# An issue order on VectorE: the second token tile's convolution taps behind the chain of its step sizes

## The chip, the cores and the metric

The kernel runs on one core of one Trainium2 chip. Its time is the device time of one execution in microseconds, given as the median of several runs. A profile is a separate execution recorded by the hardware profiler; its times are counted from the start of its span.

## What is computed

One layer of a perceiver with 256 tokens of width 512, in float32 throughout. Three blocks follow each other, each on the layer norm of the running sum x and added back to it:

```python
x = x + xattn(layernorm(x), ctx)   # attention: 16 heads over 4096 context positions and the tokens themselves
x = x + ssd(layernorm(x))          # a state space block (below)
x = x + moe(layernorm(x))          # 32 experts, 6 of them for each token, and a shared expert
```

The change lies in the second block. Cut to what matters:

```python
zxbcdt = u @ W_in.T                       # z: 1024, xBC: 1280, dt: 16 columns
xBC = silu(causal_conv(xBC, conv_w) + b)  # 4 taps along the tokens, for each of 1280 channels
dt  = softplus(dt + dt_bias)              # the step sizes: one for each token and head
A   = -exp(A_log)
dA  = dt * A;  A_cs = cumsum(dA)          # running sums inside a chunk of 128 tokens
L   = tril(exp(A_cs[l] - A_cs[s]))        # decays between two tokens of a chunk
Y   = ((C B^T) * L) @ (x dt) + C state * exp(A_cs) + x * D
y   = rmsnorm(Y * silu(z)) * norm_weight
out = y @ W_out.T
```

## The kernel before

The 256 tokens are two tiles of 128, which are the two chunks of the state space block. Attention takes about the first 720 us. The first token tile's part of the state space block up to the decays runs beside the end of attention; the second tile's part begins when its attention output has been projected and normalized, at about 737 us. The expert stage starts at about 805 us and runs to the end.

The kernel is written in a tile framework. The program names tiles and operations; the framework adds the semaphores and lays out, once at build time, the order in which each engine issues its instructions. It goes by the order of the program as priority, by the dependencies, by the free buffers, and by its own estimate of when each input is there. So an instruction that is late in the program can stand ahead of an earlier one that it expects to be not ready. `tc.issue_after(ins)` adds an order without a wait: what the block traces on the engine of `ins` is issued behind `ins` on that engine. On other engines it says nothing. On the chip each engine then works through its queue in that order.

The parts around the change, for token tile t:

- `steps_of(t)` makes the step sizes, on tiles of 128 x 16. `product` (lines 993 to 1000) turns the normalized tokens on TensorE, multiplies for dt, and prepares exp(-|v|). `series` (1002 to 1013) is the softplus as a chain of small VectorE instructions, each on the result of the one before: lines 1003 to 1007, six times line 1009, then 1010, 1012 and 1013. The last one writes dA. `sums` (1015 to 1024) makes the running sums by a matmul with a triangle (`ps_cs`) and copies them (line 1021).
- `decays(t)` spreads the sums: `ps_csT` is the transposed running sum, ScalarE copies it to `csT` and writes it to DRAM (`sums_d`), and GpSimd's queue reads it back to all partitions as `lm` (line 1039), and for the second tile also as `e1` (1043). Then come 16 subtractions on VectorE (line 1047) and the exponentials on ScalarE (1051, 1053).
- `channels(t)` is the convolution, by ten channel tiles `ct` of 128. TensorE makes a piece (`ps_xbc`); ScalarE copies it to `xraw` (1067) and writes the last tap with the bias into `y` (1068). The other three taps add to `y`: for ct 3 and 7 by ScalarE and GpSimd (1073, 1074), for the other eight by VectorE (line 1076, one instruction of 128 x 128 for each tap). `active` (1079) is the SiLU over all ten.
- `gates(t)` makes z (`ps_z`) and its SiLU on ScalarE (1091). `mixing`, `within`, `carried` and `assemble` make Y, and `mamba_out` multiplies by W_out and normalizes. `turn_xn` (234, `lnT`) turns the normalized tokens for the next block.

PSUM tiles come from three tags in a fixed rotation (`bank`): mm with two banks, sc with three, tp with one.

For the second tile the program traces, in this order:

```python
product()
series()
lm = decays(1)
run(chans[1][c] for c in order[0:3])   # channel tiles 8, 9, 0
sums()
lm[0]()                                # spread the sums
run(chans[1][c] for c in order[3:])    # channel tiles 1 to 7
run(gates(0))
run(lm[1:])                            # line 1047 and the exponentials
hold(*w_x, lacc[:, 0], behind=decay_begun[-1])
```

`hold` starts loads of expert weights on SyncE's queue (line 1427), behind the first instruction of line 1047.

Of the kernel before, what the change touches and what calls it, by code (L numbers as in the profile page):

```python
# [15 lines left out]
ALU = mybir.AluOpType  # L16
# [3 lines left out]
P = 128  # L20
# [64 lines left out]
def perceiver_layer(ctx: ExitStack, tc: tile.TileContext, a: dict, out: bass.AP):  # L85
    nc = tc.nc
    V, S, G, TE = nc.vector, nc.scalar, nc.gpsimd, nc.tensor
# [69 lines left out]
    def layer(ctx, bounded):  # L157
# [73 lines left out]
        def turn_xn(t, tp, halves=False):  # L231

            for k in range(KD):
                TE.transpose(tp[:, k * P:(k + 1) * P], xn[:, t, k * P:(k + 1) * P], ident)

            for copy, ks in (((V.tensor_copy, slice(0, KD // 2)), (S.copy, slice(KD // 2, KD))) if halves else
                             ((V.tensor_copy, slice(0, KD)),)):
                turned = copy(xT[:, ks, t * P:(t + 1) * P], tp.rearrange("p (k n) -> p k n", k=KD)[:, ks])
            return turned

        def project(ps, lhs, rhs_of):

            for k in range(KD):
                last = TE.matmul(ps, lhs(k), rhs_of(k), start=(k == 0), stop=(k == KD - 1))  # L244
            return last
# [692 lines left out]
        m = {}  # L938
        banks = ring([(ps_mm, "mm")])

        def bank(name):
            p, tag = banks()
            return p.tile([P, 512], FP, tag=tag, name=name)
# [44 lines left out]
        def steps_of(t):  # L988


            vdt, nab, u, z, z2, ser, dt, dA, acs = (m[n, t] for n in ("vdt", "nab", "u", "z", "z2", "ser", "dt", "dA", "acs"))

            def product():
                turn_xn(t, bank("lnT"), halves=True)
                ps = bank("ps_dt")
                project(ps[:, 0:SH], lambda k: xT[:, k, tok(t)], lambda k: m["w_bcd"][:, k, 256:272])
                V.tensor_tensor(vdt, ps[:, 0:SH], dt_bias, ALU.add)
                V.tensor_scalar(nab, vdt, -1.0, None, ALU.mult)
                V.tensor_tensor(nab, nab, vdt, ALU.min)
                S.activation(u, nab, AF.Exp)  # L1000

            def series():
                V.tensor_scalar(z, u, 2.0, None, ALU.add)
                V.reciprocal(z, z)
                V.tensor_tensor(z, z, u, ALU.mult)
                V.tensor_tensor(z2, z, z, ALU.mult)
                V.tensor_scalar(ser, z2, 1.0 / 15.0, None, ALU.mult)
                for d in (13, 11, 9, 7, 5, 3):
                    V.scalar_tensor_tensor(ser, ser, 1.0 / d, z2, ALU.add, ALU.mult)
                V.scalar_tensor_tensor(ser, ser, 1.0, z, ALU.add, ALU.mult)  # L1010
                V.tensor_scalar(vdt, vdt, 0.0, None, ALU.max)
                V.scalar_tensor_tensor(dt, ser, 2.0, vdt, ALU.mult, ALU.add)
                V.scalar_tensor_tensor(dA, dt, -1.0, m["ea", 0], ALU.mult, ALU.mult)

            def sums():

                ps = bank("ps_cs")
                TE.matmul(ps[:, 0:SH], upper, dA, start=True, stop=True)
                if t == 0:
                    TE.matmul(ps[:, SH:2 * SH], ones, dA, start=True, stop=True)  # L1020
                V.tensor_copy(acs, ps[:, 0:SH])
                if t == 0:
                    V.tensor_tensor(m["decay", 0], ps[:, SH:2 * SH], acs, ALU.subtract)
                    S.activation(m["decay", 0], m["decay", 0], AF.Exp)
            return product, series, sums

        decay_begun = []

        def decays(t):

# [25 lines left out]
        def channels(t):  # L1056


            xc, xraw = m["xc", t], m["xraw"]

            def piece(ct):
                w, c0 = ((w_x[ct // 4], ct % 4 * P) if ct < 8 else (m["w_bcd"], (ct - 8) * P))
                ps = bank("ps_xbc")[:, 0:P]
                project(ps, lambda k: w[:, k, c0:c0 + P], lambda k: xT[:, k, tok(t)])
                xb = xraw[:, ct, :]
                y = xc[:, ct, :]
                S.copy(xb[:, CONV - 1:], ps)
                S.activation(y, ps, AF.Identity, bias=conv_b[:, ct:ct + 1], scale=conv_w[:, ct, CONV - 1:CONV])
                for j in range(CONV - 1):
                    w = conv_w[:, ct, j:j + 1]  # L1070
                    if ct % 4 == 3:
                        tap = small.tile([P, P], FP, tag="tap", name="tap", bufs=2)
                        S.activation(tap, xb[:, j:j + P], AF.Copy, scale=w)
                        G.tensor_tensor(y, y, tap, ALU.add)
                    else:
                        V.scalar_tensor_tensor(y, xb[:, j:j + P], w, y, ALU.mult, ALU.add)

            def active():
                S.activation(xc, xc, AF.Silu)
                if t + 1 < NT:  # L1080
                    G.tensor_copy(xraw[:, :, 0:CONV - 1], xraw[:, :, P:P + CONV - 1])
            return [lambda ct=ct: piece(ct) for ct in range(XCT)], active
# [801 lines left out]
    with tc.If(flag == 1) as arms:  # L1884
        with ExitStack() as lctx:
            layer(lctx, True)
    with arms.Else():
        with ExitStack() as lctx:
            layer(lctx, False)
# [48 lines left out]
```

## Time and profile before

| what | value |
|---|---|
| median of 3 runs | 938.96 us (938.9 to 939.3) |
| the profiled execution | 939.45 us |
| its span | 937.7 us |
| TensorE busy | 924.1 us (99%) |
| VectorE busy | 579.2 us (62%) |
| ScalarE busy | 371.2 us (40%) |
| GpSimd busy | 428.3 us (46%) |
| mean granted TensorE clock | 0.998 of full speed |

In the profile PE is TensorE's matmuls and PEld its weight loads, DVE is VectorE, ACT is ScalarE, POOL is GpSimd, SP is SyncE; a q behind a name is that engine's queue of DMA issues. A float32 matmul shows as two records. A timeline line gives start, duration, engine, line, operation, out<-in by the program's names, shapes and count, and in brackets the idle time before it and what ended it. Several of the program's names share one buffer, so the 128 x 16 tiles of `steps_of` are shown as `xc`, `xraw` as `lacc`, and `e1` and z as `wkv`.

### The profile page before, as it was taken

To read this page: it belongs to the slowest core of one execution; us is meant where nothing else is said; L and a number is where in the kernel's file an instruction comes from. 1 tells how busy PE (TensorE), PEld (TensorE's weight loads), DVE (VectorE), ACT (ScalarE), POOL (GpSimd) and SP (SyncE) were. 2 spreads that over 40 slices of the span, in tenths; PEclk is the share of its full clock that TensorE was granted. 3 is DMA by queue.
4 is the path that set the end of the run, shared out by engine and by line. 5 is a ranking of instruction groups with operands and counts; after the bars stand their busy time and mean duration, and the time that the engine had idled before them with its cause. 6 is when DMAs were issued, how large, how long until landed. Compare 5 with 4: busy or idle time off the path is not lost.

```text
span 937.7 us, 10601 instructions
## 1 busy us (share of the span) xinstructions
PE 924.1 (99%) x3280; PEld 506.6 (54%) x3280; DVE 579.2 (62%) x1199; ACT 371.2 (40%) x855; POOL 428.3 (46%) x499
## 2 busy tenths in 40 slices
PE   9999999999999999999999999999999999999997
PEld 4444555555555555555555555554455695654332
DVE  4966756566665665655656666657589595662224
ACT  4556444444444343444444444434236362122211
POOL 3768855345544634725634554220003341455552
PEclk9999999999999999999999999999999999999999
DMA  9651053043015104305303401280016393689993
GB/s 335 203 113 59 0 180 89 1 129 108 12 35 179 34 12 146 91 1 157 91 0 106 109 12 35 67 268 35 0 43 200 136 332 113 233 284 352 420 392 106
DMA packets 129733, 122.33 MB, mean 130 GB/s; under 512 B 79906, under 2 KB 99139, under 8 KB 124419
## 3 DMA queue, kind: packets, MB, share of 16 engines
q1 hardware_dynamic: 118976, 77.43, 27.6%
q0 software_dynamic: 7504, 39.59, 11.4%
q10 hardware_dynamic: 3186, 4.54, 1.3%
q8 instruction: 28, 0.46, 0.2%
q14 instruction: 39, 0.31, 0.1%
HBM read 89.54 MB, written 32.00 MB: 130 GB/s over the span
## 4 chain that ended last, share of the span: by engine, by line
PE 90%; DMA 4%; DVE 4%; issue 1%; POOL 1%; ACT 0%; ACTq 0%; POOLq 0%; DVEq 0%
PE oT L787 24%; PE scT L761 24%; PE ps_kv L531 16%; PE ps_self L244 4%; PE ps_o L982 3%; PE ps_first L406 2%; PE ps_egu L244 2%; DMA xg_sb<-xd,listed 2%; DMA w_in<-in_experts_dram,place 2%; PE ps_egu L1651 1%; PE ps_xbc L244 1%; PE total L1692 1%; PE ps_ye L1722 1%; PE xgTp L1623 1%; PE ps_sgu L244 1%
## 5 line engine op out<-in xcount | busy, mean ns | idle before, releaser
L778 DVE TENSOR_TENSOR lacc<-lacc,prT 128x512 f32<-128x512 f32 x256 | 199.5, 780 | 198.4 <-ACT prT L767 197.4
L767 ACT ACTIVATE prT<-scT,bq,rk 128x512 f32<-128x512 f32 x256 | 198.5, 775 | 280.7 <-PE scT L761 269.6
L761 PE MATMUL scT<-qT,kT 128*128 128x512 f32 x536 | 273.5, 592 | 0.0
L787 PE MATMUL oT<-prT,v 128*128 128x512 f32 x528 | 269.4, 592 | 0.0
L787 PEld LDWEIGHTS oT<-prT,v 128*128 128x128 f32 x528 | 100.2, 190 | 125.3 <-issue 118.6
L761 PEld LDWEIGHTS scT<-qT,kT 128*128 128x128 f32 x536 | 101.3, 190 | 41.4 <-issue 30.8
L531 PE MATMUL ps_kv<-fast,ctx 128*128 128x256 f32 x350 | 99.5, 379 | 0.0
L531 PEld LDWEIGHTS ps_kv<-fast,ctx 128*128 128x128 f32 x350 | 66.5, 190 | 47.9 <-issue 40.2
L480 POOL TENSOR_TENSOR ctx<-ctx 128x128 f32<-128x128 f32 x21 | 10.4, 497 | 98.7 <-PE ps_kv L531 98.7
L218 POOL TENSOR_TENSOR rk<-pv,mhalf 128x4 f32<-128x4 f32 x32 | 38.4, 1211 | 27.3 <-DVE pv L217 27.1
L531 PE MATMUL ps_kv<-wkv,ctx 128*128 128x256 f32 x168 | 48.8, 379 | 0.0
L289 ACT ACTIVATE xn<-kraw 128x128 f32<-128x128 f32 x112 | 33.4, 300 | 38.6 <-POOL kraw L506 21.5
L516 POOL TENSOR_TENSOR v<-fast,v 128x768 f32<-128x768 f32 x21 | 40.9, 1959 | 16.2 <-DVE fast L560 15.6
L531 PEld LDWEIGHTS ps_kv<-wkv,ctx 128*128 128x128 f32 x168 | 31.9, 190 | 28.2 <-issue 24.4
L793 DVE TENSOR_TENSOR oacc<-oT,oacc 128x512 f32<-128x512 f32 x64 | 43.7, 682 | 0.0
L1415 POOL DMA_INDIRECT xg_sb<-xd,listed x21 | 20.4, 974 | 36.2 <-DVE lacc L1271 14.3
L531 PE MATMUL ps_kv<-fast,fast 128*128 128x256 f32 x112 | 33.3, 379 | 0.0
L531 PEld LDWEIGHTS ps_kv<-fast,fast 128*128 128x128 f32 x112 | 21.3, 190 | 17.8 <-issue 12.0
L295 DVE STREAM_TRANSPOSE tr<-kraw 128x512 f32<-128x512 f32 x28 | 18.3, 690 | 19.7 <-POOL kraw L505 19.7
L478 POOL TENSOR_TENSOR ctx<-fast 128x128 f32<-128x128 f32 x28 | 20.4, 730 | 19.5 <-PE ps_kv L531 19.1
L982 PE MATMUL ps_o<-wo,qT 128*128 128x512 f32 x64 | 28.8, 592 | 0.0
L244 PE MATMUL ps_self<-wq,xT 128*128 128x512 f32 x64 | 28.6, 592 | 0.0
(430 smaller groups left out, 1379.4 us busy)
## 6 DMA issues: line engine op xcount, KB each, us to landing
xg<-xn SPq DMA_DIRECT2D x6, 2560.0 KB, 9.1
ctx<-in_ctxT_dram SPq DMA_DIRECT2D x7, 1024.0 KB, 4.8
kd<-tr SPq DMA_DIRECT2D x112, 64.0 KB, 2.3
kT<-kd SPq DMA_DIRECT2D x28, 256.0 KB, 2.9
wq<-in_wq_dram SPq DMA_DIRECT2D x4, 1024.0 KB, 14.5
wo<-in_wo_dram SPq DMA_DIRECT2D x4, 1024.0 KB, 6.5
w_in<-in_W_inT_dram SPq DMA_DIRECT2D x4, 1024.0 KB, 5.0
w_in<-in_experts_dram SPq DMA_DIRECT2D x4, 1024.0 KB, 4.8
```

What stands on the lines that cost most here:

```text
L218: return G.tensor_tensor(dst, v[:, :n], mhalf[:, :n], ALU.pow)
L244: last = TE.matmul(ps, lhs(k), rhs_of(k), start=(k == 0), stop=(k == KD - 1))
L289: S.activation(sq[:, h, :], raw[:, h, :], AF.Square, accum_out=ss[:, h:h + 1])
L478: G.tensor_tensor(s1, x[:, 1, 0], x[:, 1, 1], ALU.add)
L516: G.tensor_tensor(to[:, 1:4], q, base[:, 1:4], ALU.add)
L531: TE.matmul(b[n], sets[name][i], y, start=start, stop=True, skip_group_check=True)
L761: scored.append(TE.matmul(sc, kT[:, g, i * P:(i + 1) * P], qT[:, t, heads4(g), :].rearrange("p h q -> p (h q)"), start=True, stop=True).ins)
L767: S.activation(pr, sc, AF.Exp, bias=shift, scale=SCALE if r is None else r[:, i, g:g + 1])
L778: V.tensor_tensor(la, la, pr, ALU.add)
L787: TE.matmul(outs[g, t], v[:, i, g * HD:(g + 1) * HD], pr, start=(n == 0), stop=last)
L793: V.tensor_tensor(ov, outs.pop((g, t)), ov, ALU.add)
L982: TE.matmul(m["ps_o", t], aT[:, t, h, :], wo[j][:, h % 4, :], start=(h == 0), stop=(h == NH - 1))
```

## The change

The instruction that writes dA is kept by its tile, and the VectorE taps of the second tile (t > 0) are traced inside `issue_after` of it. Nothing else is changed: the same instructions, the same data, the same buffers. The taps of ct 3 and 7 are outside of the block.

```diff
-                V.scalar_tensor_tensor(dA, dt, -1.0, m["ea", 0], ALU.mult, ALU.mult)
+                stepped[t] = V.scalar_tensor_tensor(dA, dt, -1.0, m["ea", 0], ALU.mult, ALU.mult).ins
...
-        decay_begun = []
+        decay_begun, stepped = [], {}
...
                     else:
-                        V.scalar_tensor_tensor(y, xb[:, j:j + P], w, y, ALU.mult, ALU.add)
+                        with tc.issue_after(stepped[t]) if t > 0 else nullcontext():
+                            V.scalar_tensor_tensor(y, xb[:, j:j + P], w, y, ALU.mult, ALU.add)
```

## The prediction

> **What bounds the kernel now.** I read the page first. TensorE (PE) is busy 924.1 of 937.7 us at the full granted clock, so only PE's idle time can be won, and what makes PE wait longer is lost. Next I read the chain of waits from 732 us on, where the second token tile's step sizes are made:
>
> ```profile
> 745.29 0.32 DVE xc L1013
> 745.65 0.40 PE ps_cs L1018 x2
> 746.05 0.32 PE ps_csT L1036 x2
> 746.37 2.00 PE ps_xbc L244 x16
> 748.37 0.22 issue
> 748.59 5.30 DMA lm<-sums
> 753.91 3.42 DVE lm L1047 x16
> ```
>
> (Start, duration, what.) The chain runs through dA (line 1013), two small matmuls, the round trip of the running sums through DRAM, and the 16 subtractions of line 1047. It then stays on VectorE (DVE) and GpSimd (POOL) up to the transposes at 780.89. DVE's own timeline in front of it shows what shares the queue with the series:
>
> ```profile
> 741.71 0.17 DVE L1006 TENSOR_TENSOR xc<-xc 128x16 f32<-128x16 f32 x1
> 741.83 0.35 DVE L1076 SCALAR_TENSOR_TENSOR xc<-lacc,by_channel,xc 128x128 f32<-128x128 f32 x1
> 742.10 0.17 DVE L1007 TENSOR_SCALAR xc<-xc 128x16 f32<-128x16 f32 x1
> ...
> 743.99 0.62 DVE L1076 SCALAR_TENSOR_TENSOR xc<-lacc,by_channel,xc 128x128 f32<-128x128 f32 x1
> 744.53 0.16 DVE L1009 SCALAR_TENSOR_TENSOR xc<-xc 128x16 f32<-128x16 f32 x1
> ...
> 746.09 0.17 DVE L1021 COPY xc<-ps_cs 128x16 f32<-128x16 f32 x1 [0.49 <-PE ps_cs L1018]
> 748.16 5.40 DVE L1076 SCALAR_TENSOR_TENSOR xc<-lacc,by_channel,xc 128x128 f32<-128x128 f32 x15 [1.90 <-ACT xc L1068]
> ```
>
> Nine of the tile's 24 VectorE taps (channel tiles 8, 9 and 0) sit one by one between the steps of the series; the other 15 run in a row before line 1047. Between the two groups DVE idles 2.4 us. Last, PE's timeline, which says how much a shorter chain can be worth:
>
> ```profile
> 743.69 1.38 PE L244 MATMUL ps_z<-xT,w_in 128*128 128x128 f32 x10 [0.72 <-ACT xc L1068]
> 745.65 0.40 PE L1018 MATMUL ps_cs<-xc,upper 128*128 128x16 f32 x2 [0.58 <-DVE xc L1013]
> ```
> ```profile
> 780.89 0.63 PE L234 MATMUL lnT<-ident,xn 128*128 128x128 f32 x4 [0.29 <-DVE xn L228]
> ```
> ```profile
> 746.00:758.00 12.00, 12.00 (x107) 11.79 (x107) 9.28 (x34) 8.05 (x20) 4.09 (x7) 1.00 0.65 209
> 758.00:770.00 12.00, 12.00 (x123) 11.71 (x122) 10.98 (x14) 8.53 (x12) 7.43 (x7) 1.00 0.91 352
> ```
>
> In the last two lines (stretch, its length, then busy time of PE, weight load, DVE, ACT, POOL, clock, DMA) PE has no hole at all from 746 to 770. So two paths run side by side to 780.89, the chain on DVE and a full PE, and they meet there 0.29 us apart. All the idle PE has near the change is 0.72 + 0.58 + 0.29 = 1.59 us.
>
> **The change, part by part.** No instruction, DMA or semaphore is added or removed. The 24 taps of the second tile get an order edge: on DVE they stand behind dA. The six taps of channel tiles 3 and 7 run on ScalarE (ACT) and POOL and get none. 15 of the 24 stand behind dA already, so nine move.
>
> *dA.* Steps of the series without a tap between them start 0.21 us apart (the four before it start at 739.70, 739.91, 740.12, 740.33). From the first step at 740.71: thirteen such spacings, plus 0.08 for the longer reciprocal, plus the last step's 0.17, give 740.71 + 2.73 + 0.08 + 0.17 = 743.69. In the trace dA ends at 745.60. So dA comes 1.9 us earlier.
>
> *PE.* The matmul of the running sums can start near 743.8 instead of 745.65. What stands ahead of it on PE decides. PE ends the four channel pieces at 742.97, and the ten gate records (ps_z) start at 743.69, when ACT frees a PSUM bank; they were put there to fill the wait for dA. If the new order sets the sums ahead of them, PE idles 743.8 - 742.97 = 0.83 instead of 0.72 + 0.58 = 1.30: gain 0.5. If they stay ahead, PE does them until 745.07 and only the 0.58 goes. Both ends agree on 0.5 to 0.6. I take 0.5, because the gate records still have to be done later. A slower PE here is excluded only if nothing else is put ahead of the sums; that is a rival.
>
> *The sums' round trip.* From dA's end to line 1047 took 753.91 - 745.60 = 8.3 us: matmul, transposed sums, the ACT copy, the write (1.9 us to POOL's issue), the read (5.3 us). ACT's third tap for channel tile 3, at 744.49 to 744.89, may stand ahead of the copy, so I allow 0 to 0.4 us. lm then lands between 743.69 + 8.3 = 752.0 and 752.4, or 753.3 if the gate records stay ahead (its issue moves with PE's 0.58). POOL's issue of lm and the two issues for e1 behind it (749.23) all move with it; e1 is first read at 762.00, so it has cover of several us.
>
> *The moved taps.* They start at 743.7 and take 0.36 each in a row (5.40 / 15): 3.2 us, to 746.9. The three POOL adds of channel tile 3 run beside them (744.00 to 745.57). The tap that began with the first add took 0.62 instead of 0.35, so 0.27 for each add, 0.8 in all: 747.7. Queued behind the taps is the copy of the sums (line 1021, 0.2), to 747.9; it was at 746.09 and is first read by line 1047, and until it is done one of the two "mm" PSUM banks stays held; of the later channel pieces only 1, 5 and 7 draw on "mm", one after the other, and the second bank serves them. The 15 later taps need ACT copies that now come about 0.5 us earlier with PE, at 747.6 for the first; so DVE goes on without a hole and ends 747.9 + 5.4 = 753.3 (753.56 before). Without any slowing by POOL it would be 752.5.
>
> [...]
>
> *Line 1047 and what follows.* It starts at the later of lm (752.0 to 753.3) and the last tap (753.3): 753.3 instead of 753.91, so 0.6 us earlier. It releases SP's first loads of expert weights (754.26 and 755.17), which come earlier by the same. The activation over all channels (line 1079) waits for the last tap but started only at 756.03, behind the gate activation, so it has 2.4 us of cover from DVE's last tap; without that cover its consumers on PE, the transposes at 757.79, would wait.
>
> *The sum.* PE arrives at 780.60 - 0.5 = 780.1 and the DVE chain at 780.89 - 0.6 = 780.3. The transposes start at about 780.3: 0.6 us earlier. Behind them PE is the chain again, and routing, gathers and expert weights start from that point, so they shift as one. The profiled execution takes 939.45 us (span 937.7 and 1.75 around it); minus 0.6 is 938.85. The median of the runs, 938.96, is 0.49 below the profiled one: **938.4 us**. About 0.2%, 1.9 us, is what a measurement can tell from no change here, so this is "within".
>
> **The rivals.**
> *Nothing arrives.* POOL's adds stop the taps altogether (1.57 instead of 0.8), the last tap ends at 754.1, and line 1047 starts where it did. PE's 0.5 is then eaten at 780.89, where it waits 0.8 for DVE. Time 939.0. For it: 0.62 us is nearly a whole add more than 0.17. Against: at 704.02 three taps beside POOL adds took 1.38 us, 0.46 each. Chance 0.10.
> *The chain's whole 1.9 us.* The chain of waits, taken alone, promises it: 937.1. It needs the last taps and PE out of the way, and PE has 1.59 us to give in all, which makes 937.4 the natural end. Only if a hole further on closes too is it more. Chance 0.08, of which 0.06 beyond the bound.
> *Taps behind the landing (slower).* The order on DVE is laid out at build time. dA is now earlier by 1.9, the later taps hardly; if the layout expects lm before the last taps, subtractions of line 1047 are set between them (in the first tile, at 715.99, one does stand between two taps), and on the chip the taps behind it stand until lm lands at 752.0 or later. With k taps behind the first subtraction the last ends at 752.0 + k x (0.36 + 0.21). The activation and the transposes on PE suffer from 757.3 - 1.26 - 0.1 = 755.9 on, so from k = 7; with all 15 behind it the end is 760.6, 4.7 us late on PE: 943. Against: in the trace all 15 stand ahead. Chance 0.10.
> *Another order in the expert stage (slower).* PE, POOL and the queues are laid out anew behind the change. POOL issues indirect loads 1.25 us apart (802.19 to 813.95), and a row load that falls behind weight loads can take 12 us to land, as the chain shows at 894.33. One or two places further back cost PE 2 to 3 us: 941 to 942. Against: all streams shift by the same 0.6, so their relations hold. Chance 0.10.
>
> **How the numbers follow.** The forecast has 0.62 and lies within 0.2%, as does the first rival (0.10) and 0.02 of the second: same 0.74. Faster 0.06, slower 0.20. The range goes from 937.1 (the second rival) to 940.8, which takes in the unknown order costs of one 1.25 us place and a little more; it leaves out most of the slower rivals and nothing else.
>
> **What would show it.** In the changed profile dA should end near 743.7 with no tap before it, the sums' matmul start at 743.8 to 745.1, nine taps follow dA and end near 747.7, the 15 later ones end near 753.3 and line 1047 start right behind; PE's two holes ahead of the sums should add to 0.7 to 0.9, and the lnT transposes start near 780.3. The prediction is wrong if subtractions stand between the last taps with a wait for lm, if PE shows a new hole at the transposes near 757.8, or if the stages behind 809 us run in another order.

## The result, and the profile after

The changed kernel takes 937.48 us (median of 22 runs, 936.09 to 938.95), the kernel before beside it 938.63 us (22 runs, 936.94 to 939.58): the ratio is 0.9988, 95% interval [0.9982, 0.9993]. That is 1.15 us less. The forecast was a median of 938.4 us, 0.56 us below 938.96, so the sign is right and the gain is twice what was forecast. The measured median lies near the lower end of the range (937.1 to 940.8), an end that came from the second rival and not from the sum. A second series with the same kernel gave 937.24 us against 938.56, ratio 0.9988 [0.9979, 0.9997].

The profiled execution took 936.52 us with a span of 934.7, which is 3.0 us less than the span before. Only a part of this belongs to the change. A measure inside the trace is cleaner: **the distance** from line 984's add of the second token tile (the last step before the changed region) to the lnT transposes behind it.

Four lines give it: VectorE's timeline (DVE) and TensorE's (PE) of the kernel before, then the same two of the changed kernel.

```profile
732.96 0.69 DVE L984 TENSOR_TENSOR x_sb<-ps_o,x_sb 128x512 f32<-128x512 f32 x1 [0.68 <-PE ps_o L982]
```
```profile
780.89 0.63 PE L234 MATMUL lnT<-ident,xn 128*128 128x128 f32 x4 [0.29 <-DVE xn L228]
```
```profile
732.19 0.69 DVE L984 TENSOR_TENSOR x_sb<-ps_o,x_sb 128x512 f32<-128x512 f32 x1 [0.68 <-PE ps_o L982]
```
```profile
778.94 0.63 PE L234 MATMUL lnT<-ident,xn 128*128 128x128 f32 x4
```

The distance is 780.89 - 732.96 = 47.93 us before and 778.94 - 732.19 = 46.75 us after: 1.18 us less, which is the gain of the medians. Of the other 1.8 us of span, 0.77 lie ahead of line 984 and 1.05 behind the transposes. The second profile of the same kernel has a span of 936.6 us and a distance of 46.77, so those parts go up and down from run to run and the distance doesn't. The kernel before has only one profile, so its 47.93 us rests on one execution; the two differences of the medians, 1.15 and 1.32 us, bear it out. Times of the changed kernel are set beside those of before by adding 0.77. Line numbers from 1076 on are one higher in it (the taps are line 1077).

VectorE's timeline after the change:

```profile
742.73 0.17 DVE L1013 SCALAR_TENSOR_TENSOR xc<-xc,xc 128x16 f32<-128x16 f32 x1
742.82 2.32 DVE L1077 SCALAR_TENSOR_TENSOR xc<-lacc,by_channel,xc 128x128 f32<-128x128 f32 x7
745.07 0.16 DVE L1021 COPY xc<-ps_cs 128x16 f32<-128x16 f32 x1
745.18 5.16 DVE L1077 SCALAR_TENSOR_TENSOR xc<-lacc,by_channel,xc 128x128 f32<-128x128 f32 x17
751.84 3.50 DVE L1047 TENSOR_SCALAR lm<-lm,xc 128x128 f32<-128x128 f32 x16 [1.50 <-DMA lm<-sums]
```

The series ends at 742.90 without a tap in it. Seven taps follow, then the copy of the sums, then 17 taps without a hole to 750.34. The new thing is the last bracket: VectorE now stands idle for 1.50 us until lm lands. Before, that wait was 0.35 us. TensorE's timeline after the change:

```profile
742.96 0.40 PE L1018 MATMUL ps_cs<-xc,upper 128*128 128x16 f32 x2 [0.76 <-DVE xc L1013]
743.28 0.39 PE L1036 MATMUL ps_csT<-upper,xc 128*16 128x128 f32 x2
743.61 5.62 PE L244 MATMUL ps_xbc<-xT,w_in 128*128 128x128 f32 x48
```

The ten gate records (ps_z) that stood ahead of the sums' matmul are gone from there; they run later, with the other gate records. One hole of 0.76 us is left. From 742.96 to the transposes no wait shows on TensorE, and at the transposes there is no bracket any more. The chain of waits of the changed kernel says the same (start, duration, what):

```profile
743.68 5.55 PE ps_xbc L244 x48
749.23 7.15 PE ps_z L244 x64
...
773.78 5.25 PE ps_out L1177 x12
779.03 0.55 PE lnT L234 x4
```

Before, the chain left TensorE at 748.37 for the round trip of the sums and stayed on VectorE and GpSimd, but for one step of 0.64 us on ScalarE, to 780.89. Now it stays on TensorE all the way. The two stretches that were shown before (stretch, its length, busy time of PE, weight load, DVE, ACT, POOL, clock, DMA) are as full on TensorE as they were, at the same clock:

```profile
746.00:758.00 12.00, 12.00 (x110) 12.00 (x110) 10.36 (x34) 8.42 (x17) 6.09 (x9) 1.00 0.81 282
758.00:770.00 12.00, 12.00 (x112) 10.81 (x111) 10.96 (x15) 6.98 (x11) 6.82 (x7) 1.00 0.88 329
```

### The profile page after: what moved, and what is told of

The parts are those of the page before. It is cut to its first block, busy times and chain, and to the rows that moved or that the text cites. A ratio compares the mean times of both kernels' runs of the same rounds, so it can differ in the third digit from the quotient of the medians.

```text
span 934.7 us, 10600 instructions
## 1 busy us (share of the span) xinstructions
PE 922.4 (99%) x3280; PEld 506.4 (54%) x3280; DVE 578.1 (62%) x1199; ACT 371.0 (40%) x855; POOL 429.0 (46%) x499
## 4 chain that ended last, share of the span: by engine, by line
PE 95%; DVE 2%; DMA 1%; issue 0%; ACT 0%; POOL 0%; ACTq 0%; POOLq 0%
PE oT L787 24%; PE scT L761 24%; PE ps_kv L531 16%; PE ps_self L244 4%; PE ps_o L982 3%; PE ps_egu L244 3%; PE ps_egu L1652 2%; PE ps_first L406 2%; PE ps_xbc L244 2%; PE ps_z L244 2%; PE ps_out L1177 2%; DMA xg_sb<-xd,listed 1%; PE xgTp L1624 1%; PE ps_ye L1674 1%; PE total L1693 1%; PE ps_ye L1723 1%
## 5 line engine op out<-in xcount | busy, mean ns | idle before, releaser
L531 PE MATMUL ps_kv<-wkv,ctx 128*128 128x256 f32 x168 | 48.8, 379 | 0.0
```

The source lines that it names most:

```text
L531: TE.matmul(b[n], sets[name][i], y, start=start, stop=True, skip_group_check=True)
```

## The experiments

The theory: the change wins by a shorter wait of TensorE ahead of the sums, and by the earlier lm that takes VectorE's chain off the transposes; both paths must give. The rivals: it is the other order on TensorE that wins (it moved five gate matmuls, ten records), or the chain of dA in full, or nothing of this and only scatter.

**e1: TensorE's order alone.** The kernel before, with the gates' matmuls held behind the transposed sums; VectorE keeps its taps in the series.

```diff
...
-                TE.matmul(ps, m["dA", t], upper, start=True, stop=True)
+                spread_on[t] = TE.matmul(ps, m["dA", t], upper, start=True, stop=True).ins
...
-                    project(ps[:, tok(i)], lambda k: w_z[j][:, k, tok(i)], lambda k: xT[:, k, tok(t)])
+                    with tc.issue_after(spread_on[1]):
+                        project(ps[:, tok(i)], lambda k: w_z[j][:, k, tok(i)], lambda k: xT[:, k, tok(t)])
```

> The kernel before with one edge on TensorE alone: the gate products of the first tile stand behind the transposed running sums (ps_csT), as they do after the change; VectorE's queue up to dA is that of before, nine taps between the steps. All runs are read by the distance D from the start of the add of line 984 (second token tile) to the start of the next lnT transposes: 47.93 us before (732.96 to 780.89), 46.75 after (732.19 to 778.94). Theory (an earlier dA takes idle time out of TensorE's queue): dA stays late, TensorE idles from the fourth channel piece to the sums, and the ten gate records (1.12 us at 0.112 each) are done later: TensorE comes to lnT 1.12 later than its 780.60, D 48.7 to 48.8, time 0.8 us above before. Rival (the new order on TensorE is what brings the gain): D near 46.8, time 1.1 us below before.

Measured: 941.33 us (6 runs) against 938.29, ratio 1.0033 [1.002, 1.0045]. The distance is 51.82 us. The direction was expected, the size was not: 3 us more than any theory gave. TensorE's timeline of e1:

```profile
744.63 0.61 PE L1018 MATMUL ps_cs<-xc,upper 128*128 128x16 f32 x2 [2.68 <-DVE xc L1013]
745.17 0.61 PE L1036 MATMUL ps_csT<-upper,xc 128*16 128x128 f32 x2
745.71 8.33 PE L244 MATMUL ps_xbc<-xT,w_in 128*128 128x128 f32 x48
```

The hole of 2.68 us is as expected. But the same 48 records that take 5.62 us in the changed kernel take 8.33 us here, and the two small matmuls 0.61 instead of 0.40 and 0.39: 2.71 + 0.43 = 3.14 us more. Against the expected 48.7 to 48.8 that is the whole excess. So either the order itself makes them slow, or something that follows from the hole does. The granted clock in short stretches of e1 (stretch, its length, then busy time of PE, weight load, DVE, ACT, POOL, then clock, DMA share and GB/s) speaks for the second:

```profile
744.50:744.75 0.25, 0.12 (x1) 0.12 (x1) 0.08 (x1) 0.00 (x0) 0.04 (x1) 0.68 0.00 0
744.75:745.00 0.25, 0.25 (x2) 0.25 (x2) 0.00 (x0) 0.00 (x0) 0.00 (x0) 0.50 0.00 0
...
751.25:751.50 0.25, 0.25 (x3) 0.25 (x3) 0.07 (x1) 0.25 (x2) 0.00 (x0) 0.67 1.11 459
751.50:751.75 0.25, 0.25 (x4) 0.25 (x4) 0.00 (x0) 0.25 (x2) 0.00 (x0) 1.00 1.23 459
```

**e9: e1 with its hole filled.** Eight matmuls of a constant behind channel tile 3's piece (`last` is the last matmul of that piece, `full` its bank); nothing uses their product.

```diff
...
+                if t > 0 and ct == 3:
+                    with tc.issue_after(last.ins):
+                        for _ in range(8):
+                            TE.matmul(full[:, P:2 * P], ones, ones, start=True, stop=True)
```

> The kernel of e1 (the order of before on VectorE, the five gate matmuls held behind the sums on TensorE), with eight extra matmuls of a constant on TensorE between the fourth channel piece and the matmul of the sums; their product is not used. Counted at the 0.112 us of each of their 16 records they take 1.8 us, so e1's hole of 2.68 us shrinks to about 0.9 us, and nothing that anyone waits for moves: dA comes when it came. Theory: e1 lost 3.1 us more than its hole because TensorE's granted clock fell to 0.50 after the long hole (745 to 751.5 us in that run); without the long hole the clock stays at 1.00, the next 48 records of the channel pieces take 5.6 us instead of 8.3, and the distance from line 984's add (second tile) to the next lnT transposes is 48.7 us (e1: 51.82 us, before: 47.93 us). Rival: the slow matmuls come from the order itself (banks that ACT frees later, or weights that arrive late); then they stay at 0.17 us a record and the distance is 51.5 to 52 us.

Measured: 938.70 us (10 runs) against 938.47, ratio 1.0004 [0.9994, 1.0013]; the distance is 48.88 us, where 48.7 was expected. More work on TensorE made the kernel 2.8 us faster than e1, each against the kernel before beside it (3.04 and 0.23 us above). The clock over the same stretch, first of e1, then of e9:

```profile
745.00:751.00 6.00, 6.00 (x29) 5.55 (x29) 1.97 (x7) 1.51 (x5) 2.07 (x3) 0.50 0.29 86
```
```profile
745.00:751.00 6.00, 6.00 (x57) 6.00 (x56) 4.56 (x14) 4.67 (x17) 3.43 (x6) 1.00 0.28 82
```

In 6 us TensorE is busy throughout in both; it gets 29 records done at a clock of 0.50 and 57 at 1.00. The 48 records of the pieces take 5.62 us again. One part of the expectation missed: dA came 0.56 us earlier than in e1, since GpSimd's adds, which ran beside the series in e1, come behind it here; TensorE reached the transposes by 48.20 us and waited 0.68 for VectorE. Without that lead TensorE would have come by 48.8, still what the theory said; that the distance itself came so near to 48.7 is partly luck, since VectorE set it. The rival (the order itself) is out: the loss beyond the hole is the granted clock after the hole. And TensorE's new order, without the new order on VectorE, brings no gain even with the clock at 1.00.

**e2: VectorE's order alone.** The changed kernel with the ten gate records back ahead of the sums. The piece of channel tile 3 and the begun gate take a bank out of turn, so that the rotation stays as it was; `z_part` issues matmuls 0 to 4 of a gate.

```diff
...
-        sums()
-        lm[0]()
-        run(chans[1][c] for c in order[3:])
+        chans[1][3]((ps_tp, "tp"))
+        z_begun[0, 1] = bank("ps_z", (ps_tp, "tp"))
+        with tc.issue_after(z_part(z_begun[0, 1], 0, 1, 0, 5).ins):
+            sums()
+            lm[0]()
+        with tc.issue_after(spread_on[1]):
+            for c in order[3:]:
+                chans[1][c]() if c != 3 else banks()
```

> The changed kernel with TensorE's order of before: five gate matmuls (ten records) are held ahead of the running sums; VectorE's queue is that of after, no tap ahead of dA. Theory (two paths that meet at lnT, TensorE's full queue and VectorE's chain from the sums): dA ends 1.9 us earlier than before, the sums start when the gate records are done, 0.8 us earlier than before and 1.1 later than after. TensorE comes to lnT as early as after, but the sums' round trip is later by 1.1 less the 0.5 that GpSimd's queue held it up after the change, so line 1047 and with it lnT are 0.2 to 0.7 earlier than before: D 47.2 to 47.7, time 0.2 to 0.7 below before. Rival (TensorE's idle time alone counts): D 46.8, 1.1 below. Rival (dA alone counts, wherever the sums stand): D 46.8 as well, and then line 1047 starts as early as after the change.

Measured: 937.00 us (11 runs) against 938.29, ratio 0.9991 [0.9982, 1.0]; the distance is 47.25 us. So 0.68 of the 1.18 us come from VectorE's order by itself, within the 47.2 to 47.7 that was expected. By its time (1.29 us below before, interval 0 to 1.7) e2 can't be told from the changed kernel; the distance tells them apart. What limits e2 stands at the transposes:

```profile
778.77 0.63 PE L234 MATMUL lnT<-ident,xn 128*128 128x128 f32 x4 [0.46 <-DVE xn L228]
```

TensorE waits 0.46 us for VectorE's chain there. The matmul of the sums stands behind the ten records and starts 743.46 - 731.52 = 11.94 us after line 984, where it takes 12.69 before and 10.77 in the changed kernel; lm comes later by it, and line 1047 starts 20.26 us after line 984 (20.95 before, 19.65 changed). So neither order alone explains the result: alone, TensorE's order loses and VectorE's gains 0.68; together they gain 1.18 in the distance.

**e3: half of the chain.** The taps are held only behind the third of the six steps of line 1009.

```diff
-                    V.scalar_tensor_tensor(ser, ser, 1.0 / d, z2, ALU.add, ALU.mult)
+                    step = V.scalar_tensor_tensor(ser, ser, 1.0 / d, z2, ALU.add, ALU.mult).ins
+                    if d == 9:
+                        stepped[t] = step
...
-                stepped[t] = V.scalar_tensor_tensor(dA, dt, -1.0, m["ea", 0], ALU.mult, ALU.mult).ins
+                V.scalar_tensor_tensor(dA, dt, -1.0, m["ea", 0], ALU.mult, ALU.mult)
```

> The changed kernel, the taps behind the third of the six steps of line 1009 instead of behind dA. Six of nine taps stay between steps, three gate matmuls stand ahead of the sums on TensorE. Theory: each tap taken out is worth 1.9 / 9 = 0.21 us of dA, so dA is 0.6 earlier than before relative to the add of line 984; TensorE gains 0.2 and the lnT hole of 0.29 closes: D 47.4 to 47.5. Rival (the gain comes from the whole block of taps being off the queue, not tap by tap): D as before, 47.9, or as after, 46.8.

Measured in one run: 937.17 us; the distance is 47.13 us. dA starts 743.52 - 731.92 = 11.60 us after line 984 (before 12.33, after 10.54), so 0.73 us earlier where 0.6 was expected, and the distance gains 0.80 where 0.4 to 0.5 was. Less than half of dA's advance brings two thirds of the gain: the gain doesn't follow dA one to one. Six of the ten gate records stay ahead of the sums here, so only four are put off: TensorE gains 4.72 - 3.84 - 4 x 0.112 = 0.43 us from its first w_in piece to the sums, and with the 0.37 us of waiting at the transposes that the next section works out, that is the 0.80.

**e4: the edge in both tiles.** `if t > 0` is dropped.

```diff
-                        with tc.issue_after(stepped[t]) if t > 0 else nullcontext():
+                        with tc.issue_after(stepped[t]):
```

> The changed kernel with the same order for the first token tile too (its taps behind its dA). There TensorE is full of attention beside the chain. Theory: the first tile's dA and running sums come 1 to 2 us earlier, nobody on TensorE waits for them, and D stays 46.7 to 46.8; time as after the change (0.0 +- 0.3 us). Rival (the chain is worth its length wherever it stands): 1 us or more faster than after. Rival (taps late): the activation over the first tile's channels comes later and the transposes behind it on TensorE wait; 0.5 us or more slower.

Measured: 937.40 us (11 runs) against 938.29, ratio 0.9994 [0.9985, 1.0003]; the distance is 46.76 us, as expected. The first tile's dA does come earlier: it starts 732.96 - 703.94 = 29.02 us ahead of line 984 in the kernel before, and 733.03 - 701.95 = 31.08 us here. The distance begins behind it and can't show what that is worth; the time can, and the rival's further 1 us lies outside its interval. In the kernel before TensorE is busy for 37.00 of the 37 us from 695 to 732, so there is no idle time that an earlier dA could take.

**after_again: the changed kernel once more,** on the chip of the three experiments that follow.

> The changed kernel itself beside the two versions of this call, on the same chip. Theory: D 46.7 to 46.8 again, and 1.0 to 1.3 us below before; the part of the profiled difference of 3.0 us that lies outside D (0.77 ahead of line 984, 1.05 behind lnT) varies from run to run and is not the change's. Rival: the part behind lnT is the change's too, and the time is 2 us or more below before.

Measured: 937.24 us (11 runs) against 938.56, 1.32 us less; the distance is 46.77 us. The part behind the transposes is 156.8 us, as before the change (the first profile of the changed kernel had 155.8), so it is not the change's.

**e5: the last hole filled.** Channel tile 1 is traced ahead of the sums, and the sums stand behind the last matmul of its piece (`pieced`). TensorE then has 20 instead of 16 records of w_in pieces ahead of the sums, 0.45 us more work in the 0.76 us.

```diff
...
-        run(chans[1][c] for c in order[0:3])
-        sums()
+        run(chans[1][c] for c in order[0:4])
+        with tc.issue_after(pieced[1, 1]):
+            sums()
         lm[0]()
-        run(chans[1][c] for c in order[3:])
+        run(chans[1][c] for c in order[4:])
```

> The changed kernel with channel tile 1 traced ahead of the sums and held there on TensorE, so two more channel matmuls (0.45 us) stand in the hole of 0.76 us that is left ahead of the sums. Side effects of the new layout: only one of GpSimd's adds of channel tile 3 stands ahead of its read of the sums, and on ScalarE the first square of line 1169 stands ahead of the activation over all channels (line 1080). Theory: that square waits for line 1047 and line 1168 on VectorE, so the activation moves from 754.50 to about 756.05 (on the changed kernel's clock) and the transposes of xc on TensorE from 756.2 to about 757.3: the cover that the forecast named is gone, TensorE gets a hole of 1.4 us there, D 47.6 to 47.8, time 1.0 us above the changed kernel. Rival (the work put into the hole is what counts): D 46.3 to 46.45, 0.4 below the changed kernel.

Measured: 941.02 us (8 runs) against 938.56, ratio 1.0026 [1.0015, 1.0036]; the distance is 50.57 us. The cover of the activation over all channels is gone, as the theory said. ScalarE's and TensorE's timelines of e5:

```profile
756.03 0.63 ACT L1169 ACTIVATE ctx<-qT 128x512 f32<-128x512 f32 x1 [2.40 <-DVE qT L1168]
756.57 1.25 ACT L1080 ACTIVATE xc<-xc 128x1280 f32<-128x1280 f32 x1
```
```profile
757.88 1.97 PE L1102 MATMUL xtT<-ident,xc 128*128 128x128 f32 x8 [2.60 <-ACT xc L1080]
759.64 0.64 PE L1112 MATMUL ps_g<-xc 128*128 128x128 f32 x2
760.07 7.65 PE L244 MATMUL ps_z<-xT,w_in 128*128 128x128 f32 x64
```

ScalarE has a square (line 1169) ahead of the activation, and the square waits 2.40 us for VectorE; so the transposes xtT wait 2.60 us for the activation, where they wait for nothing in the changed kernel. The price is again larger than the hole. The xtT transposes take 1.97 us instead of 1.04, ps_g 0.64 instead of 0.39, the gate records 7.65 instead of 7.31: 1.43 us by differences of starts (0.89 + 0.21 + 0.33). The fill itself won 0.38: the gate records ahead start at 747.97 and take 7.15 by their spacing, so TensorE was ready for xtT 755.12 - 731.47 = 23.65 us after line 984, where the changed kernel takes 24.03. Counted from there the wait is 2.76 us (the bracket counts from 755.28, where the profile's model lets the last record end). 2.76 + 1.43 - 0.38 is 3.81; the distance is 50.57 - 46.75 = 3.82 us longer. The clock in two stretches of e5, where it falls and where it returns:

```profile
757.25:757.50 0.25, 0.00 (x0) 0.00 (x0) 0.00 (x0) 0.25 (x1) 0.00 (x0) 0.70 1.16 492
...
760.75:761.00 0.25, 0.25 (x4) 0.25 (x4) 0.25 (x2) 0.25 (x2) 0.00 (x0) 0.97 0.17 66
```

**e5d: the same with the activation's cover put back.** e5, with the activation traced ahead of `assemble(0)`, the squares behind it, and the gate's activation behind channel tile 7's taps on ScalarE.

```diff
...
+        silu[1]()
         assemble(0)
...
-        silu[1]()
...
-                S.activation(sq[:, cols], flat(y[:, cs, :]), AF.Square)
+                with tc.issue_after(activated[-1]):
+                    S.activation(sq[:, cols], flat(y[:, cs, :]), AF.Square)
```

> As e5_fill_the_hole, with ScalarE's order mended: the squares stand behind the activation over all channels, and the gate activations behind the scaled taps of channel tile 7. Theory (two paths meet at lnT): TensorE is 0.45 us earlier by the filled hole, VectorE's chain 0.3 to 0.5 earlier because GpSimd's read of the sums no longer stands behind an add: D 46.3 to 46.45, time 0.3 to 0.45 us below the changed kernel. Rival (something else bounds, as the 0.4 us the forecast gave to TensorE alone): D 46.7, no change.

Measured: 936.92 us (11 runs) against 938.56, ratio 0.9984 [0.9975, 0.9993]; the distance is 46.57 us where 46.3 to 46.45 was expected. TensorE reaches xtT 0.38 us earlier against line 984, but the transposes start 0.70 us after the record ahead of them, where it is 0.51 in the changed kernel: 0.19 us of waiting for VectorE's chain. lm's read was not issued earlier, as was expected: an add of GpSimd (746.94) still stands ahead of it (747.45), and line 1047 starts 19.65 us after line 984 as in the changed kernel. It is the best version here, and beats the kernel before; from the changed kernel (937.24 in the same series) it can't be told apart by its time.

**e6d: lm's read earlier, alone.** The changed kernel, with GpSimd's third add of channel tile 3 behind the read, and e5d's mends on ScalarE.

```diff
...
-                        G.tensor_tensor(y, y, tap, ALU.add)
+                        with tc.issue_after(read_on[t]) if t > 0 and ct == 3 and j == CONV - 2 else nullcontext():
+                            G.tensor_tensor(y, y, tap, ALU.add)
```

> The changed kernel with GpSimd's third add of channel tile 3 behind its read of the sums, and ScalarE's order as in e5d_fill_with_cover; TensorE's order is that of the changed kernel. Theory: the read is issued 0.3 to 0.5 us earlier and line 1047 starts as much earlier, but TensorE's queue is full to lnT, so D stays 46.7 to 46.8. Rival (VectorE's chain alone sets lnT): D 46.3 to 46.4.

Measured in one run: 937.51 us; the distance is 46.77 us. VectorE's timeline of e6d (two lines) and TensorE's, with line 984 at 731.30:

```profile
749.86 3.65 DVE L1047 TENSOR_SCALAR lm<-lm,xc 128x128 f32<-128x128 f32 x16 [0.22 <-DMA lm<-sums]
...
774.82 0.75 DVE L1188 SCALAR_TENSOR_TENSOR x_sb<-ps_out,ry,x_sb 128x512 f32<-128x512 f32 x1 [1.72 <-PE ps_out L1180]
```
```profile
778.07 0.63 PE L234 MATMUL lnT<-ident,xn 128*128 128x128 f32 x4
```

Line 1047 starts 18.56 us after line 984, 1.1 us earlier than in the changed kernel, where 0.3 to 0.5 was expected (the read was issued 0.48 us sooner after the matmul of ps_csT, and landed in 4.85 us instead of 5.47). The transposes gain nothing. The add into x_sb, from which the last layer norm ahead of the transposes starts, waits here for TensorE's product ps_out. So after the change TensorE's own queue sets the transposes, and a still earlier lm is worth nothing by itself.

What stays open: an earlier lm together with a filled hole. It wasn't tried.

## Why the prediction was right, and where its sizes were off

The case that was forecast is the one that came: a gain within 0.2%, because two paths meet at the transposes and both have to give. The sum said 0.6 us, the distance says 1.18; both terms of the sum were too small, and the path that sets the end was the other one. By its steps, with 0.77 added to the times after:

- *dA.* Forecast end 743.69; measured 742.90, that is 743.67. The spacing of 0.21 us was the right price, and no tap stands ahead.
- *What stands ahead on TensorE.* The gate records went behind the sums, as the first of the two cases had it; the matmul of the sums starts at 743.73 and its hole is 0.76 (forecast 0.83).
- *TensorE's gain: mis-sized, 0.5 forecast, 0.80 measured.* From the start of the channel pieces of w_in to the sums took 745.65 - 740.93 = 4.72 us before and 742.96 - 740.16 = 2.80 after. Of the 1.92 us, ten gate records of 7.15 / 64 = 0.112 us are only put off: 1.12. So 0.80 is won. The prediction took the two brackets, 0.72 + 0.58, for all the idle time. But the group of ten records between them is shown with 1.38 us, of which only 1.12 is work; the rest is the end of the last one as the profile models it. The idle time was 1.56 (0.80 won, 0.76 left), not 1.30.
- *The round trip.* Forecast for lm 752.0 to 753.3; measured 751.84, that is 752.61. Of dA's 1.93 us, 0.63 were lost in it: the read was issued 746.37 - 744.00 = 2.37 us after the write instead of 748.59 - 746.69 = 1.90, behind the third add on GpSimd's queue (from the start of the matmul of ps_csT it is 3.09 us instead of 2.61, and in e6d, with that add behind the read, 745.01 - 742.40 = 2.61 again), and took 5.47 us to land instead of 5.32. The prediction had looked for such a delay on ScalarE, not on the queue that issues the read:

```profile
745.86 0.53 POOL L1074 TENSOR_TENSOR xc<-xc,tap 128x128 f32<-128x128 f32 x1 [0.87 <-ACT tap L1073]
746.37 0.64 POOL L1039 DMA_DIRECT2D lm<-sums  x1
```

- *The moved taps: the step that was wrong.* The last tap was forecast at 753.3, and was to set line 1047. It ended at 750.34, that is 751.1, and lm sets line 1047. The 24 taps took 7.5 us, 0.31 each instead of 0.36. The price of 0.36 us holds for the order in which the 15 taps ran before: in threes, with starts 0.39, 0.39 and 0.27 us apart. ScalarE's copies did not pace them: they come 0.89 us apart, VectorE takes 1.04 for three taps, and its last three start at 752.31, when ScalarE had written their input by 751.70. In the changed kernel most taps start 0.26 us after the one ahead, before that one, of 0.34 to 0.35 us, has ended. That the three taps of a group were on one tile, and that the new order alternates between tiles, is the author's guess: the traces do not name the channel tile. And the 0.8 for GpSimd's adds was too much: the adds no longer ran in one row (their ScalarE taps were spread, and they came at 743.23, 744.41 and 745.86), and each made one tap 0.54 us long instead of 0.34, 0.6 in all. So line 1047 came 20.95 - 19.65 = 1.30 us earlier after line 984, not 0.6.
- *The transposes.* Forecast 780.3; measured 778.94, that is 779.71. Here too the modelled end of the records hides idle time. From the start of the twelve ps_out records ahead to the transposes it was 780.89 - 775.21 = 5.68 us before and is 778.94 - 773.63 = 5.31 after, so the wait that is gone is 0.37, not 0.29. TensorE's 0.80 and this 0.37 make 1.17 of the 1.18. That the last wait is gone, and TensorE the bound, was not forecast; it was to be VectorE by 0.2 us. VectorE's path has little to spare, though: its add into x_sb starts 2.21 us behind the matmul ps_ss both in e6d, where TensorE's ps_out ends its wait, and in the changed kernel, where GpSimd's step ry does (at 775.71). So after the change the two paths arrive almost together. In e5d, which won 0.38 us on TensorE, ry ends that wait too, 2.41 us behind ps_ss, and the distance gained only 0.18.

The rivals. "Nothing arrives" had GpSimd's adds stop the taps altogether. The row of 0.62 us that spoke for it is 0.27 more than the 0.35 of the taps around it, half an add of 1.57 / 3 = 0.52; the 0.17 that it was set against is the time of a 128 x 16 step, not of a tap. After the change, seven taps beside two adds took 2.32 us, 0.33 each, and twelve without an add (e5d) 3.23, 0.27 each; in e2 seven taps beside three adds in a row took 2.66, so an add cost 0.2 to 0.26 us, near the 0.27 that was forecast. Taps that stood still for both adds would have taken 0.52 + 0.58 = 1.10 us more; they took 2.32 - 7 x 0.27 = 0.43 more. The trace shows a slowing, not a full stop. "The whole 1.9" didn't come because an earlier dA is worth only the idle time that it takes out of TensorE: 0.80 + 0.37 us, with 0.76 left in the hole. e6d shows it directly: 1.1 us more on VectorE's chain gave nothing. "Taps behind the landing" didn't happen, but its place was right: the activation and the transposes xtT are where e5 lost 2.60 us. "Another order in the expert stage" didn't happen: TensorE, VectorE, GpSimd and SP work there in the order of before.

## What to carry to other kernels

When two paths meet at one instruction, price both, and take work between two holes by the duration of one record times their number, not by the group's span: the modelled end hides idle time (here ten records were shown with 1.38 us, of which 1.12 was work). A group's mean held here only for the order in which the group ran: the taps took 0.36 us each in one order and 0.31 in another, 0.27 where no add ran beside them. If the change sets a new order, give such a price a range. And before work is moved out of a hole, see how long a hole it leaves: the same move of gate matmuls that pays with a hole of 0.76 us cost 3.14 us extra with one of 2.68.

## What the runs showed of the hardware

The holes of 2.68 us (e1) and 2.60 us (e5) on TensorE were paid for twice, as idle time and again in the slow stretch behind them: 3.14 us in e1 and 1.43 us in e5. In e1 the engine ended its pieces at 741.95 by the profile, and the granted clock fell from 1.00 to 0.50 at about 744.6, after some 2.6 us without a matmul; it was back at 1.00 at 751.4, 6.8 us later. In e5 it fell from 1.00 to 0.50 at about 757.35, 2.1 us after the last matmul, and was back at 760.77, 3.4 us later (the edges are worked out from the mean clock of the quarter of a microsecond in which they fall). With holes of 0.35 us (e9, clock over 743 to 752), 0.72 and 0.58 us (the kernel before, 742 to 752) and 0.76 us (the changed kernel, 742 to 752) it stayed at 1.00. From how long a hole on the clock falls, these runs do not show. The mean granted clock of a whole execution is 0.994 to 0.997 over e1's six and 0.996 to 0.998 over e5's eight, against 0.997 to 0.999 for the changed kernel, so the slow stretch does not seem to be equally long in every execution, and the prices worked out for e1 and e5 are those of the profiled execution.
